# Four PSUM banks lent to the first and last side jobs of a Mamba phase, and its weight parts made in the phase ahead

## The chip, the cores and the metric

The kernel runs on one core of a Trainium2 chip. The metric is the device time of one execution in microseconds (us), and the value compared is the median of several runs. One run of the kernel before was also recorded by the hardware profiler; all times of single instructions come from that one.

The engines are called as in the profile: PE (TensorE, matrix products and transposes; PEld are its weight loads), DVE (VectorE), ACT (ScalarE), POOL (GpSimd) and SP (SyncE, which here issues every DMA). PE writes only to PSUM, whose eight banks hold 512 float32 numbers in each of 128 partitions.

## The reference, cut to what matters

The input is a batch of 8 feature maps of 256 channels, 32 by 32. Four layers follow each other: attention with a gated FFT feed-forward block; channel-group attention with a small MLP; an 8-bit quantised residual block of three convolutions; and a four-direction Mamba block. The change lies at the seam between the third and the fourth layer and at the end of the fourth, which computes for each of the four scan directions of each sample:

```python
xz = u @ W_in.T                                   # u: (1024, 256), W_in: (1024, 256)
x, z = jnp.split(xz, 2, axis=-1)
xc = conv1d_depthwise(x, conv_w, 4 taps) + conv_b
x = silu(xc)
x_dbl = x @ W_x.T                                 # 16 for dt, 16 for B, 16 for C
dt = softplus(x_dbl[..., :16] @ W_dt.T + b_dt)
A = -exp(A_log)                                   # 512 channels x 16 states
h_t = h_{t-1} * exp(dt_t A) + dt_t B_t x_t        # a scan over 1024 positions
y_t = sum over states of h_t C_t
y = (y + x * D) * silu(z)
out = y @ W_out.T
```

The four outputs, turned back to the layout of the image, are added.

## The kernel before

**Phase A** (`phase_a`) does layers 0 to 2 for all samples. Its last product is a tensor of 8-bit codes in DRAM for each sample. **Phase B** (`phase_b`) is the Mamba layer. The pools of the two phases use the same SBUF and PSUM, so that phase B starts when phase A has finished.

**The order of work.** In each phase every job is a Python generator ("strand") that yields its instructions one by one, or a condition that it waits for. The planner `_Order` holds for every instruction a cost and for every tile the time of its last use; at each step it picks, among the strands that are ready, the instruction that could start first, and between equals the one of the lowest rank. What it picks is emitted at once. On the chip each engine works through its own list strictly in this order, and SP its list of DMAs. Tiles come from a `_Room`, a fixed number of buffers of one shape; `take` waits until one is left. In phase A `fill` puts filler matmuls (tile `minus`) into the places where the planner sees PE waiting, one for every 0.3 us.

**Phase B** cuts the 1024 positions of each direction of each sample into two halves of 512. One half of one direction is a block; there are 64. A block has 16 groups, one for each state, and a group has four scans, one for each 128 channels. The stream of a block is: `scales` (ACT and POOL: dt·x times B, tile `dbu`), `turns` (PE: into bank `db`), `decays` (ACT: `da`), `scans` (DVE: `h`), `products` (POOL: times C, which `rows` loads into `cb`), `sums` (PE: adds over the states in four banks). The stream waits for nothing but its data; in its gaps the side jobs for later blocks run, which `ahead` hands to the planner at set places: `inputs` (the projections of W_in into `xi`), `mixed` (convolution, silu, W_x), `steps` (dt and `du`), and, after a sample's last direction, `fold` (the sums back to the channel layout), and `outputs` (the gate's projections, and W_out).

**The banks.** Phase B divides the eight banks so: `py_room` has 4, which `sums` holds for a block or a pair of blocks; `ps_room` (tag `db`) has 3; and `pp_room` has one, through which every side job passes:

```python
py_room = _Room(banks, "py", TH, [P, DI])
ps_room = _Room(banks, "db", 3, [P, HALF])
pp_room = _Room(banks, "pp", 1, [P, HALF])
```

**The head of phase B.** `W_in` is used as three bfloat16 parts, whose sum is the float32 weight. Ahead of everything else phase B loads each of the 8 pieces of 128 outputs (`da`), splits it on DVE (a cast, a subtraction, a cast, a subtraction, a cast, into `dbu`) and stores the parts to DRAM (`w_in`). A projection loads its parts from there into one of two `wi` tiles and multiplies them with `xf`, the codes of half an image as bfloat16, of which there is one tile. Then come `inputs` of the first sample (8 projections), `mixed(0)`, `steps(0)` and `mixed(1)`, all from the start and all through the one pp bank, and the stream begins when block 0 has its `du`.

**The tail.** After the last block's sums DVE adds the four py banks into `yT`, four folds follow (four transposes and one addition each), then for each half four gates (a projection, two instructions on DVE, three on ACT, one on POOL; two tiles `z`) and two products with W_out, each copied by ACT to a `z` tile and stored.

Most instructions of the phases are emitted by `_Op.emit`, so that the profile shows them all at line 132; they are told apart by their tiles. The loop that splits the weights is at lines 1163 to 1172.

## Time and profile before

| | us |
|---|---|
| median of 3 runs | 10775.12 |
| lowest and highest of them | 10765.92, 10776.5 |
| the profiled execution | 10771.94 |
| its span | 10770.2 |
| first DMA of phase B | 3683.84 |
| first projection | 3699.72 |
| first dbu | 3808.18 |
| first scan | 3811.12 |
| end of the last scan | 10708.15 |
| DVE's first addition of the last sums (yT) | 10711.78 |
| ACT's last copy | 10766.53 |

The span runs from the first to the last recorded instruction, and 1.7 us of the profiled time lie around it. Phase A takes the first 3683 us, the 64 blocks of the stream 6897 us (107.8 each), the head 127 us and the tail 59 us.

How to read the views: the page gives the busy time of each engine over the whole span, and a row of 40 slices. A table of windows gives the same for chosen stretches, with the clock that the throttle granted to PE (1.00 is full). The instructions in order of time show for each its start, its duration (of a run of equal ones, from the first start to the last end), and in brackets how long the engine had been idle before it and which instruction ended the wait. "pp<-xf,wi" writes tile pp from xf and wi.

### The profile page before, as it was taken

How to read it: one execution, taken by the hardware profiler on the slowest of the kernel's cores; microseconds unless marked ns; L12 is line 12 of the kernel's file. 1: busy time of each engine (PE TensorE's matmuls, PEld its weight loads, DVE VectorE, ACT ScalarE, POOL GpSimd, SP SyncE). 2: the span in 40 equal slices, each digit the busy share in tenths (PEclk: the TensorE clock that was granted, in tenths of full speed). 3: DMA queues.
4: the chain of work that ended last, by engine and by line, in shares of the span. 5: the costliest groups of instructions: out<-in, count | busy, mean ns of one | idle time of the engine just before them, and what ended most of it. 6: DMA issues, size and time to landing. Idle time of an engine off the chain costs nothing. (4 is left out here: it accounts for less than half of the span.)

```text
span 10770.2 us, 157247 instructions
## 1 busy us (share of the span) xinstructions
PE 9924.2 (92%) x58586; PEld 6252.6 (58%) x58698; DVE 8478.2 (79%) x8992; ACT 8690.8 (81%) x16283; POOL 6733.0 (63%) x3745
## 2 busy tenths in 40 slices
PE   9999999999999889999999999999989999999998
PEld 3333333333333267777777777777777777777776
DVE  5266557577665379898998998998899899899897
ACT  7867676777767488888888888888888888888887
POOL 1432133132220178888888888888888888888887
PEclk7988999989999899999999999999999999999999
DMA  1000000000000011111111111111111111111111
GB/s 46 29 18 16 22 16 22 13 22 12 13 13 10 30 41 39 50 48 50 48 46 52 50 41 55 41 50 53 44 49 52 47 48 46 52 50 43 55 41 47
DMA packets 217345, 410.00 MB, mean 38 GB/s; under 512 B 24881, under 2 KB 69297, under 8 KB 211458
## 3 DMA queue, kind: packets, MB, share of 16 engines
q1 hardware_dynamic: 216578, 399.94, 12.0%
q8 instruction: 461, 7.55, 0.3%
q14 instruction: 306, 2.51, 0.1%
HBM read 358.43 MB, written 30.93 MB: 36 GB/s over the span
## 5 line engine op out<-in xcount | busy, mean ns | idle before, releaser
L132 POOL TENSOR_TENSOR h<-h,cb 128x1024 f32<-128x1024 f32 x2048 | 4873.9, 2395 | 899.6 <-ACT st L132 445.5
L132 ACT ACTIVATE da<-dt,am 128x512 f32<-128x512 f32 x4096 | 2869.3, 713 | 505.9 <-DVE h L132 497.4
L132 DVE TENSOR_TENSOR_SCAN h<-da,st,db 128x512 f32<-128x512 f32 x2048 | 2467.2, 1257 | 167.9 <-PE db L132 92.7
L132 DVE TENSOR_TENSOR_SCAN h<-da,db 128x512 f32<-128x512 f32 x2048 | 2346.1, 1198 | 230.7 <-PE db L132 152.0
L132 ACT ACTIVATE dbu<-du,bT 128x512 f32<-128x512 f32 x3584 | 2474.9, 709 | 34.1 <-PE db L132 31.8
L132 PE MATMUL db<-ident,dbu 128*128 128x128 f32 x14336 | 2219.6, 280 | 165.0 <-DVE h L132 134.6
L132 PE MATMUL py<-ident,h 128*128 128x128 f32 x16384 | 2121.1, 275 | 93.9 <-POOL h L132 86.2
L132 PEld LDWEIGHTS db<-ident,dbu 128*128 128x128 f32 x14336 | 1672.9, 143 | 694.4 <-DVE h L132 364.2
L132 PEld LDWEIGHTS py<-ident,h 128*128 128x128 f32 x16384 | 1842.4, 141 | 171.5 <-POOL h L132 140.7
L132 DVE TENSOR_REDUCE stats<-bank 128x1 f32<-128x512 f32 x1536 | 981.5, 681 | 747.5 <-PE bank L132 746.4
L132 ACT ACTIVATE bank<-bank,stats 128x512 f32<-128x512 f32 x1536 | 1023.0, 669 | 391.2 <-DVE stats L132 380.9
L132 POOL TENSOR_TENSOR mid<-mid,mid 128x961 f32<-128x961 f32 (+2 forms) x192 | 401.2, 2097 | 1046.9 <-ACT mid L132 676.9
L132 PE MATMUL pp<-xi,cvd 128*128 128x512 f32 x2048 | 953.3, 609 | 9.6 <-ACT xs L132 3.4
L132 PE MATMUL bank<-big,big 32*128 32x512 f32 x4096 | 908.5, 670 | 36.5 <-ACT bank L132 17.9
L132 ACT ACTIVATE exps<-bank 128x512 f32<-128x512 f32 x1536 | 797.4, 621 | 137.6 <-PE bank L132 133.2
L132 PE MATMUL db<-dg,du 128*128 128x128 f32 x4096 | 811.0, 280 | 0.0
L132 POOL TENSOR_TENSOR dt<-dt,tmp 128x512 f32<-128x512 f32 x512 | 652.0, 1273 | 173.8 <-DVE tmp L132 151.0
L132 DVE TENSOR_TENSOR tmp<-dt,xs 128x512 f32<-128x512 f32 x256 | 604.2, 2360 | 194.3 <-POOL dt L132 194.1
L132 PEld LDWEIGHTS db<-dg,du 128*128 128x128 f32 x4096 | 638.0, 197 | 0.0
L132 PEld LDWEIGHTS pp<-xi,cvd 128*128 128x128 f32 x2048 | 380.8, 196 | 406.4 <-issue 391.9
L132 DVE SCALAR_TENSOR_TENSOR mid<-mid,cols,mid 128x961 f32<-128x961 f32 (+1 forms) x384 | 603.7, 1572 | 6.7
L132 PEld LDWEIGHTS bank<-big,big 32*128 32x128 f32 x4096 | 284.7, 192 | 499.2 <-issue 247.9
(186 smaller groups left out, 11280.3 us busy)
## 6 DMA issues: line engine op xcount, KB each, us to landing
cb<-c_d SPq DMA_DIRECT2D x1024, 256.0 KB, 3.2
wi<-w_in SPq DMA_DIRECT2D x192, 192.0 KB, 3.4
big<-in_x_dram SPq DMA_DIRECT2D x16, 1024.0 KB, 5.6
kept<-big SPq DMA_DIRECT2D x16, 1024.0 KB, 4.0
big<-kept SPq DMA_DIRECT2D x16, 1024.0 KB, 4.9
cdb<-codes SPq DMA_DIRECT2D x48, 256.0 KB, 4.1
big<-big SPq DMA_DIRECT2D x16, 512.0 KB, 7.2
out_dram<-z SPq DMA_DIRECT2D x32, 256.0 KB, 2.5
```

What stands on the lines that cost most here:

```text
L132: return getattr(getattr(nc, self.engine), self.method)(*self.args, **self.kw)
```

## The change

Phase A gets one strand more, `weight_parts`, of the lowest rank (9; the samples have 2). It does the loads, splits and stores of the weights that stood at the head of phase B, in two of phase A's seven `low` tiles, wherever the planner finds room. The DRAM tiles of the parts are made ahead of both phases.

In phase B a list `spare` decides which room a side job takes its bank from: `lend` takes from the four py banks as long as the list holds them, and from the single pp bank otherwise. It holds them from the start until block 0 has all its `du`, and again from the moment at which the last group's sums have left their banks. `sums` takes its four banks only when the first product of its block is there. `mixed(1)` is no longer started at once, but by `behind`, when block 0 has its `du` and the py banks are taken back. Every side job asks `lend` in place of `take(pp_room)`, and gives its bank back to the room that it came from.

```diff
-    phase_a(tc, i, col, ident, codes)
-    phase_b(tc, i, col, ident, codes, out)
+    parts = [dram.tile([P, CC, 3, P], BF16, name=f"w_in{m}", tag=f"w_in{m}") for m in range(2 * DC)]
+
+    phase_a(tc, i, col, ident, codes, parts)
+    phase_b(tc, i, col, ident, codes, parts, out)
...
+    def weight_parts():
+        for m, to in enumerate(w_parts):
+            w = yield from take(low, [P, CC, P])
+            o = yield from take(low, [P, CC, 3, P], BF16)
+            yield S.dma_start(w, i["w_in"].rearrange("(k p) m -> p k m", p=P)[:, :, m * P : (m + 1) * P])
+            for e in range(3):
+                yield V.tensor_copy(o[:, :, e], w)
+                if e < 2:
+                    yield V.tensor_tensor(w, w, o[:, :, e], ALU.subtract)
+            yield S.dma_start(to, o)
+            put(low, w)
+            put(low, o)
+
     with tc.manual_schedule():
         for b in range(B):
             order.add((2, b), sample(b))
+        order.add((9, B), weight_parts())
         order.run()
...
-    w_parts = [dr.tile([P, CC, 3, P], BF16, name=f"w_in{m}", tag=f"w_in{m}", bufs=1) for m in range(2 * DC)]
-    for m in range(2 * DC):
-        w, o = da_room.take([P, CC, P]), db_room.take([P, CC, 3, P], BF16)
-        nc.sync.dma_start(w, i["w_in"].rearrange("(k p) m -> p k m", p=P)[:, :, m * P : (m + 1) * P])
-        for e in range(3):
-            nc.vector.tensor_copy(o[:, :, e], w)
-            if e < 2:
-                nc.vector.tensor_tensor(w, w, o[:, :, e], ALU.subtract)
-        nc.sync.dma_start(w_parts[m], o)
-        da_room.put(w), db_room.put(o)
...
+    spare = [py_room]
+
+    def lend():
+        room = spare[0] if spare else pp_room
+        t = yield from take(room, [P, HALF])
+        return room, t
...
-            ps = yield from take(pp_room)
+            room, ps = yield from lend()
...
-            put(pp_room, ps)
+            put(room, ps)
...
             if s == 0 and fresh:
-                py = yield from takes(TH, py_room)
+                py = yield from takes(TH, py_room, when=lambda: (g, 0) in scaled)
...
                     put(py_room, py[t])
+                if g == len(groups) - 1:
+                    spare.append(py_room)
...
+    def behind(jobs):
+        d, h = blocks[0]
+        yield lambda: {("du", c) for c in range(DC)} <= d.done[h]
+        spare.clear()
+        for j in jobs:
+            order.add((0, 0), j)
+
-    for f in (list(inputs(0, False, xis[0, False])), mixed(0), steps(0), mixed(1)):
+    for f in (list(inputs(0, False, xis[0, False])), mixed(0), steps(0), [behind(mixed(1))]):
         for j in f:
             order.add((0, -1), j)
```

## The prediction

> **What bounds the kernel now.** I read the page first, then a table of windows by stage, then the instructions in order of time at the two places that the change touches.

> ```profile
> PE 9924.2 (92%) x58586; PEld 6252.6 (58%) x58698; DVE 8478.2 (79%) x8992; ACT 8690.8 (81%) x16283; POOL 6733.0 (63%) x3745
> ...
> PE   9999999999999889999999999999989999999998
> ```

> TensorE looks busy everywhere, but a slice is 269 us wide and hides both ends of the Mamba phase. The windows (engines in the header's order, then granted clock, DMA share and GB/s) show them:

> ```profile
> core 0: us, PE busy (x) PEld busy (x) DVE busy (x) ACT busy (x) POOL busy (x), PEclk, DMA share, GB/s
> 3683.80:3811.10 127.30, 78.00 (x168) 27.95 (x170) 30.19 (x70) 34.09 (x52) 31.51 (x45) 0.71 0.16 49
> 3811.10:3912.60 101.50, 92.01 (x622) 74.05 (x622) 86.78 (x78) 90.84 (x173) 82.96 (x46) 0.97 0.12 38
> 10421.40:10523.80 102.40, 92.81 (x642) 73.07 (x643) 94.68 (x83) 89.33 (x146) 90.03 (x50) 1.00 0.14 43
> 10523.80:10614.50 90.70, 78.98 (x593) 69.32 (x592) 88.47 (x81) 84.41 (x162) 86.55 (x47) 0.94 0.15 44
> 10711.70:10770.20 58.50, 33.97 (x98) 13.66 (x98) 17.87 (x24) 18.49 (x30) 10.12 (x8) 0.85 0.13 43
> ```

> The first row is the head: 127 us before the first scan, with every engine but TensorE three quarters idle. The last row is the tail, 58.5 us with all of them idle for long. The three between are single blocks of the stream (64 scans each), where four engines are near 90% and work is well overlapped. In head and tail one chain sets the time:

> ```profile
> 3683.84 2.43 SPq L1166 DMA_DIRECT2D da<-in_w_in_dram  x5
> ...
> 3699.72 0.59 PE L132 MATMUL pp<-xf,wi 128*128 128x512 bf16 x1 [31.88 <-DMA w_in<-dbu]
> ...
> 3703.28 2.72 PE L132 MATMUL pp<-xf,wi 128*128 128x512 bf16 x6 [0.84 <-DVE xi L132]
> ...
> 3739.67 3.67 PE L132 MATMUL pp<-xi,cvd 128*128 128x512 f32 x8 [0.87 <-ACT xs L132]
> ```

> ```profile
> 10715.90 1.11 PE L132 MATMUL pp<-ident,yT 128*128 128x128 f32 x4 [1.11 <-DVE ys L132]
> ...
> 10762.73 3.70 PE L132 MATMUL pp<-ys,w_o 128*128 128x512 f32 x8 [0.68 <-ACT z L132]
> ```

> Each bracket is a wait for the one pp bank: TensorE fills it, idles until DVE or ACT has emptied it, fills it again. The first bracket is another wait: the weight parts have to be split and stored before the first projection.

> **The change, part by part.** The profiled execution took 10771.94 us (span 10770.2), 3.2 below the median of 10775.12; I sum against the former and take the same difference off the median. The build's order of instructions says what moved: 48 projections, 16 conv matmuls, all of w_x, w_dt and transposes of block 0 now write py, and so do the tail's; DVE's order is the same from the third block to the end, bank names apart.

> *Head.* Before, from the timeline: start 3683.84, first projection 3699.72 (15.9), first conv 3728.39 (28.7), last xs done 3748.61 (20.2), xd done 3758.47 (9.9), first w_dt 3763.73 (5.3), last du done 3808.15 (44.4): 124.3 us.
> - Weight parts gone from here: 24 casts, 16 subtractions, 16 DMAs. SP issues w_x, w_o, w_dt (some 0.45 each), then cdb; its landing took 3.4 (3694.87 to 3698.23) and TensorE began 1.5 later. With 0.6 for the 512 KB of w_o ahead of it: 6.8 instead of 15.9. POOL's cvd, dd and memsets end at 3701.3, and the convs start after that: hidden.
> - Eight projections in four banks: DVE no longer gates them. At half clock 2.72 each back to back, plus 1.4 where the second half's xf is cast: 23.2. At full clock 1.46 each (as at 10731.16), but two wi tiles with a landing of 2.4 allow one per 2.0: 18.3 with a cold start. I take 20, plus 0.9 to the convs: 20.9 (28.7).
> - Convs: 4 x 3.67, then 0.7 for the last eviction: 15.4 (20.2). A cold start adds 2.2.
> - Table load 1.28, four silus 2.19, last w_x pair 0.9, xd 0.7, and 0.9 for half of a cold w_x (5.53 against 3.63): 6.0 (9.9). Transposes of xd: 0.5 (5.3, which held a conv of mixed(1)).
> - dt: one channel block goes w_dt to POOL's end in 6.2 (3763.73 to 3769.90), then multiply, transposes and copy, 0.7 each: 8.4. ACT needs 3.05 for each. tmp has three tiles and each takes two, so the third starts when the first is transposed (+7.7), the fourth some 3.3 later, and the last ends at 19.7. Bounds: 17.6 (ACT alone) to 26.9 (one after the other).

> Sum 69.3, so 55 less; 3 off for hand-overs that I don't see: **52** (42 to 58).

> *mixed(1) moved into block 0.* What filled the head's gaps now runs in the stream. Price by rows: the blocks at 10421.40 and 10523.80 both host a steps job, and only the first a mixed one: 102.4 against 90.7, so 11.7. The upper end is TensorE's own time, 4 x 3.67 + 3.63 = 18.3, since block 0 already has TensorE at 92.0 of 101.5 and would reach 110. The lower end is nothing, if it all falls into idle time. Queued behind its jobs are steps(1) and mixed(2), in the same bank. I take **14**, a third of the way up from the row.

> *Tail.* Four folds, each 2.2 apart, become DVE-bound at 1.06, so the gate projections start at 10718.1 instead of 10722.7. A gate's z goes DVE 0.75, ACT 1.95, POOL 1.26, some 4.1 with hand-overs, and z has two tiles. With that and the wi landings the fourth gate ends at 10730.6 (10740.0). The out projections take 0.9 + 3.7 (the first three quarters of the first are done by then), four more projections and gates follow to 10749.5, because the second store on SP now stands behind two wi loads and holds a z tile; then 0.9 + 3.7, copy 0.6 and store 3.1: 10758 instead of 10770.2. So **12**. At half clock throughout (2.72 and 5.5) I get 3.5; 15 if the store doesn't hold z.

> *Weight parts in the first phase.* By the rows 24 casts of 0.331 and 16 subtractions of 0.432, 14.9 us of DVE. By the order, part 0 stands ahead of the first layer norm (x lands at 20.5 to 25.7, DVE starts at 28.0), part 1 inside it, where DVE is the chain, parts 2 to 5 among the first softmax maxima, 6 and 7 at some 290 to 400 us, where DVE is nearly idle. SP gets 16 DMAs; its stores wait for DVE, and behind them stand two of the transfers big<-big. I count part 1 (1.9) and half of parts 2 to 5 (3.7): **6** lost. All of it exposed is 14.9. The clock also plays here:

> ```profile
> 100.00:230.00 130.00, 126.50 (x327) 40.92 (x324) 79.41 (x139) 102.31 (x271) 31.63 (x14) 0.61 0.06 16
> 230.00:480.00 250.00, 247.15 (x1250) 82.86 (x1248) 57.89 (x96) 203.15 (x365) 99.13 (x49) 1.00 0.12 32
> ```

> TensorE is the bound at a clock of 0.61; ten us more or less of half clock are worth 5. Ends: 8 gained, 20 lost. The two low tiles lent and 28 more filler matmuls show that this stretch's order shifts.

> 52 - 14 + 12 - 6 = **44 us**: 10728 in the profile, **10731** as median.

> [...] The row first, projections in one bank (clock in the third figure from the right):

> ```profile
> 3699.70:3728.30 28.60, 21.52 (x47) 0.50 0.20 59
> 3728.30:3732.80 4.50, 4.41 (x6) 0.50 0.00 0
> 3732.80:3766.90 34.10, 25.05 (x58) 1.00 0.09 25
> ```

> TensorE busy 75% of the time stayed at half clock for 28.6 us, and 4.5 us without a gap brought it to full. Back-to-back projections look like the second row, so I give them the full clock after some 4 us. [...]

> **The rivals.**
> 1. *The first phase takes it back.* All 14.9 us of DVE exposed and 30 us more of half clock at 100 to 300 us: 30 lost instead of 6, gain 20, 10755. For: DVE is in the chain from 28 to 50 us. Against: after 50 us it waits 95 us for TensorE in the first 300.
> 2. *Block 0 chokes on its one bank.* Hold times: conv 4.5, w_x 5.3 with its transposes, dt 4.6. Two mixed and one steps make 65 us of a block of 115; if the busy engines stretch each hold 2.2 times, 140, and block 1 waits 25 us: gain 19, 10756. Against: blocks with inputs, mixed and steps pass in 107.5.
> 3. *Slower: the clock drops in the first attention.* From 230 to 480 us TensorE is busy 247 of 250 us at clock 1.00. Every us of that at half clock costs half a us. From 132 of the 250 us on, 66 are lost and the kernel is 22 slower: 10797. Against: the order there is nearly the same and DVE has 58 of 250 us busy.

> That the change doesn't do what it says is excluded by the order.

> **How the numbers follow.** A measurement tells 0.2%, 21.5 us, from no change. Forecast 0.82; rival 1 0.07, rival 2 0.06 (both within 0.2%), rival 3 0.05. Half-widths: head 8, block 0 9, tail 6, first phase 14; together, as independent, 19, stretched to 26 to take in the two rivals inside 0.2%: 10706 to 10758.

> **What would show it.** Right: first projection some 7 us after the phase's first DMA; projections without waits for DVE xi; first scan some 50 us sooner after that DMA; block 0 at 113 to 118 us; the last store some 46 us after the last sums. Wrong: the phase's first DMA later than 3700 (rival 1); a wait of DVE scans for dbu or du ahead of block 1 (rival 2); a clock below 1.00 between 230 and 480 (rival 3).

## The result, and the profile after

The changed kernel took 10706.29 us (median of four runs, 10696.43 to 10710.81); the kernel before, run beside it, took 10775.81. The ratio is 0.9939, with a 95% interval of 0.9923 to 0.9955: faster by 0.6%, as forecast in sign. The forecast time of 10731 was 25 us too long, and the measured one lies at the very low end of the range (10706). The profiled execution of after took 10710.81 us (span 10708.9), the longest of the four.

The page of after, its first line of busy times and its row of PE slices, to set against the first fence of the prediction:

```profile
PE 9899.2 (92%) x58614; PEld 6251.0 (58%) x58726; DVE 8487.3 (79%) x8991; ACT 8702.0 (81%) x16284; POOL 6736.6 (63%) x3746
...
PE   9999999999999899899999999999989999998998
```

It hardly shows a change: the same work, the same shares, the row ends in 8998 where it ended in 9998. The gain lies again in stretches much shorter than a slice. The windows of head, block 0 and tail of after (columns as before):

```profile
core 0: us, PE busy (x) PEld busy (x) DVE busy (x) ACT busy (x) POOL busy (x), PEclk, DMA share, GB/s
3674.80:3747.30 72.50, 47.42 (x130) 19.37 (x132) 15.93 (x27) 24.90 (x39) 25.75 (x43) 0.77 0.17 50
3747.30:3857.10 109.80, 103.53 (x650) 75.40 (x648) 91.05 (x82) 97.54 (x181) 83.34 (x46) 1.00 0.11 35
10666.30:10708.90 42.60, 32.25 (x97) 14.42 (x97) 17.68 (x24) 18.21 (x30) 10.16 (x8) 0.87 0.19 59
```

The head shrank from 127.3 to 72.5 us, the tail from 58.5 to 42.6. Block 0 grew from 101.5 to 109.8, with TensorE now busy for 103.5 of it: the convolutions that left the head are there. Put together from the two profiles:

| stage (us) | before | after | gain | forecast |
|---|---|---|---|---|
| first phase, up to the first DMA of phase B | 3683.8 | 3674.9 | 9.0 | -6 |
| head, to the first scan | 127.3 | 72.4 | 54.8 | 52 |
| blocks 0 to 3 | 418.8 | 432.8 | -14.0 | -14 |
| blocks 4 to 63 | 6478.2 | 6482.6 | -4.4 | 0 |
| from the last scan's end to the end | 62.1 | 46.2 | 15.8 | 12 |
| sum | 10770.2 | 10708.9 | 61.3 | 44 |

The instructions of after's head in order of time, PE's and SP's first one:

```profile
3674.85 0.38 SPq L1173 DMA_DIRECT2D w_x<-in_w_x_dram  x1
...
3682.51 0.59 PE L134 MATMUL py<-xf,wi 128*128 128x512 bf16 x1 [23.67 <-ACT xf L134]
...
3690.07 1.47 PE L134 MATMUL py<-xf,wi 128*128 128x512 bf16 x6 [1.01 <-DMA wi<-w_in]
3692.30 1.46 PE L134 MATMUL py<-xf,wi 128*128 128x512 bf16 x6 [0.75 <-ACT xf L134]
...
3699.15 13.90 PE L134 MATMUL py<-xi,cvd 128*128 128x512 f32 x32
...
3741.06 5.64 PE L134 MATMUL pp<-xi,cvd 128*128 128x512 f32 x8
3746.54 0.49 PE L134 MATMUL db<-ident,dbu 128*128 128x128 f32 x3
```

The brackets have changed. In before they named DVE or ACT, emptying the one bank; now the projections wait for their weights (`wi`) and for the cast of the input (`xf`), and the four convolutions run as one row of 32 matmuls without a gap. One bracket in the head still reads `[0.81 <-DVE xi]`, ahead of the seventh projection at 3696.20; the weight load that starts with it waited for `wi`, and with two banks the wait at this place reads `[0.66 <-DMA wi]`, so it too goes with the weights. The last two lines show something that the forecast lacked: a convolution of `mixed(1)`, released when block 0 has its `du`, got onto TensorE's list ahead of the first `db`, so that the first scan comes 5.3 us after the last `du`, where it came 3.0 after it before.

In the tail, gate products and out products follow each other without bank waits. The two longest waits of DVE now end when a store frees a `z` tile:

```profile
10669.35 4.10 DVE L134 TENSOR_TENSOR ys<-py,ys 128x512 f32<-128x512 f32 x4 [0.57 <-PE py L134]
...
10679.45 7.26 PE L134 MATMUL py<-ys,w_o 128*128 128x512 f32 x16
...
10688.60 0.75 DVE L134 TENSOR_SCALAR z<-py,cols 128x512 f32<-128x512 f32 x1 [6.78 <-DMA out_dram<-z]
...
10692.69 0.75 DVE L134 TENSOR_SCALAR z<-py,cols 128x512 f32<-128x512 f32 x1 [2.67 <-DMA out_dram<-z]
```

Of the 6.78 only some 0.6 are the store's: up to 10686.7 TensorE was at the out products, and the projection that this gate reads ended at 10688.0. The 2.67 are the store's whole.

### The profile page after: what moved, and what is told of

Same layout as the page of the kernel before. It is cut to its first block, busy times and chain, and to the rows that moved or that the text cites. A ratio compares the mean times of both kernels' runs of the same rounds, so it can differ in the third digit from the quotient of the medians.

```text
span 10708.9 us, 157325 instructions
## 1 busy us (share of the span) xinstructions
PE 9899.2 (92%) x58614; PEld 6251.0 (58%) x58726; DVE 8487.3 (79%) x8991; ACT 8702.0 (81%) x16284; POOL 6736.6 (63%) x3746
## 5 line engine op out<-in xcount | busy, mean ns | idle before, releaser
L134 PE MATMUL pp<-xi,cvd 128*128 128x512 f32 x2016 | 930.6, 605 | 3.5 <-DVE dt L134 1.5
```

The costliest lines, as they stand in the source:

```text
L134: return getattr(getattr(nc, self.engine), self.method)(*self.args, **self.kw)
```

## The experiments

The profiles left three questions. Which part of the head's gain is the banks', which the weights', and which the later `mixed(1)`? Is the shorter first phase the weights' doing, or only a luckier execution? And why did TensorE's clock come up so much sooner than in before (1.47 us for each projection from the fourth on, where all eight of before took 2.72)?

Theory A: the terms are separate, and the weight parts in the first phase cost nothing there, since their order also changes how long TensorE runs at half clock. Rival B: the shorter first phase is the spread between executions. Rival C: the weight work is hidden wherever it stands. Rival D: the blocks after the head are slower for another reason than the moved work. All stages of all whole kernels, from one profile each (us):

| kernel | first phase | head | blocks 0-3 | blocks 4-63 | after the last scan |
|---|---|---|---|---|---|
| before | 3683.8 | 127.3 | 418.8 | 6478.2 | 62.1 |
| warm-up only | 3670.9 | 121.1 | 419.4 | 6484.6 | 62.2 |
| weights only | 3677.3 | 109.6 | 419.1 | 6488.2 | 62.5 |
| banks only | 3702.7 | 81.6 | 426.4 | 6478.7 | 44.5 |
| mixed(1) at once | 3687.9 | 82.6 | 422.7 | 6477.9 | 44.6 |
| after | 3674.9 | 72.4 | 432.8 | 6482.6 | 46.2 |
| weights late | 3691.3 | 71.4 | 426.4 | 6485.4 | 45.7 |
| two banks | 3672.0 | 72.9 | 426.4 | 6474.9 | 45.0 |
| wide | 3665.8 | 68.0 | 426.4 | 6478.9 | 38.6 |

Head and tail repeat within 1 or 2 us between kernels that share their code there. The first phase does not: before, warm-up only and banks only have the same instructions in it in the same order, and took 3683.8, 3670.9 and 3702.7 us. So totals are compared as ratios to runs of before beside them (whose median was 10760.55 in one group and 10776.83 in another), and stages by the profile.

**Weights only.** The parts are made in the first phase; head and tail keep their one bank, and `mixed(1)` starts at once.

```diff
-        room = spare[0] if spare else pp_room
+        room = pp_room
...
-                py = yield from takes(TH, py_room, when=lambda: (g, 0) in scaled)
+                py = yield from takes(TH, py_room)
...
-    for f in (list(inputs(0, False, xis[0, False])), mixed(0), steps(0), [behind(mixed(1))]):
+    for f in (list(inputs(0, False, xis[0, False])), mixed(0), steps(0), mixed(1)):
```

> Only the weight parts move to the first phase; every side job keeps the one bank. Theory A (the three terms are separate, and the first phase is shorter because the shifted order at its start brings the full clock earlier): the first phase has the changed kernel's order, so it is 9 us or more shorter than before again; the head loses the wait for the split weights, 15.9 down to 7.7; blocks and tail as before. Total 10776 - 9 - 9 = 10758, down to 10750. Rival B (the 9 us of the first phase were one execution's luck, and the weight work costs the 6 us that I forecast): 10776 + 6 - 9 = 10773.

Measured: 10761.13 us, ratio 0.9989 (0.998 to 0.9998). The head is 17.7 us shorter than before's, where the first projection comes only 8.2 sooner (7.65 us after the phase's first DMA instead of 15.9). Nearly all of the rest is TensorE's clock. The projections in order of time:

```profile
3684.94 2.72 PE L134 MATMUL pp<-xf,wi 128*128 128x512 bf16 x6 [23.65 <-ACT xf L134]
3688.50 1.45 PE L134 MATMUL pp<-xf,wi 128*128 128x512 bf16 x6 [0.84 <-DVE xi L134]
3690.80 1.46 PE L134 MATMUL pp<-xf,wi 128*128 128x512 bf16 x6 [0.84 <-DVE xi L134]
```

One bank, the same wait of 0.84 us for DVE as in before, and yet 1.46 us each from the second on, where all eight of before took 2.72: 19.8 us to the first convolution instead of 28.7. The clock of the profiles changes on a grid of 3.41 us: of the 224 stretches of one clock in before's records and the 216 in after's, all but the last of each, which the end of the record cuts off, are whole multiples of 3.413 us long. Windows on that grid, first of before, then of weights only (a step is "filled" by the share of it in which matmuls ran):

```profile
3702.09:3705.51 3.42, 2.58 (x7) 0.83 (x6) 0.75 (x1) 0.00 (x0) 0.00 (x0) 0.50 0.22 58
3705.51:3708.92 3.41, 2.57 (x7) 0.70 (x6) 0.75 (x1) 0.00 (x0) 0.00 (x0) 0.50 0.42 135
```

```profile
3684.80:3688.22 3.42, 2.72 (x6) 0.87 (x7) 0.53 (x1) 0.48 (x1) 3.42 (x7) 0.50 0.00 0
3688.22:3691.63 3.41, 2.29 (x10) 0.96 (x10) 0.97 (x2) 0.00 (x0) 2.25 (x13) 1.00 0.36 102
3691.63:3695.04 3.41, 2.08 (x9) 0.68 (x7) 1.21 (x2) 0.41 (x1) 0.00 (x0) 1.00 0.45 148
```

Before filled its steps to 0.75 and stayed at half clock; this kernel's first projection happened to fall whole into one step, filled it to 0.80, and the steps after it were at full clock with only 0.61 to 0.67 filled. So 8.8 of the 17.7 us in this one profile come with a clock that rose after the first projection; whether its place on the grid decided it was not shown. The total is nearer to A's 10758 than to B's 10773, but not for A's reasons: in the profile the first phase is 6.5 us shorter (A: 9 or more), the head 17.7 (A: 9), and blocks 4 to 63 are 10.0 longer.

**Banks only.** The weight parts are made at the head of phase B again, all else as in after.

```diff
-        order.add((9, B), weight_parts())
...
+    for m in range(2 * DC):
+        w, o = da_room.take([P, CC, P]), db_room.take([P, CC, 3, P], BF16)
...
+        da_room.put(w), db_room.put(o)
```

> Only the banks are lent; the weight parts are made at the head of the Mamba phase as before, and the first phase has the order of before. Theory A: head 55 less the 8 that the weights were worth, so 47 gained; blocks 0 to 3 lose 14 to 18; tail gains 16; first phase nothing: 10776 - 47 + 16 - 16 = 10729. Rival B gives the same here; if the total comes out at 10715 or below, the first phase's part of the gain isn't the weights' doing at all.

Measured: 10707.5 us (10703.74 to 10735.7), ratio 0.9944 (0.9931 to 0.9957). The head is 81.6 us, so that the weights' part of after's head is 9.2 us (the forecast's 15.9 to 6.8 is 9.1). By the expectation's rule a total of at most 10715 spoke against the weights having shortened the first phase. But the profiled execution is the slowest of the five, with a first phase of 3702.7 us, so that this total could not decide it; the runs of the first phase alone, below, were made for that.

**Weights late.** The strand waits until the fifth sample has passed its first stage.

```diff
     def weight_parts():
+        yield lambda: stage[4] >= 1
```

> The changed kernel, but the weight parts wait until sample 4 has passed its first layer, so that the first phase starts in the order of before. Theory A (order at the start sets the clock there): the half clock of the first 250 us comes back to some 123 us from 99, and the first phase is 9 or more longer than in the changed kernel: 10716 to 10722. Rival C (the weight work is simply hidden wherever it stands, and the first phase is faster for another reason): as the changed kernel, 10706.

Measured: 10728.99 us (10710.41 to 10747.42), ratio 0.9963 (0.9949 to 0.9976). Head and tail are those of after; the first phase took 3691.3 us. C, by which the place of the work makes no difference, expects after's time; this is 23 us above it. It is also above A's 10716 to 10722, and A's reason did not show: TensorE was at half clock for 96 us of the first 250, not for some 123 (after: 99).

**mixed(1) at once.** The four banks are lent, but the convolutions of block 1 start with those of block 0.

```diff
-    for f in (list(inputs(0, False, xis[0, False])), mixed(0), steps(0), [behind(mixed(1))]):
+    for f in (list(inputs(0, False, xis[0, False])), mixed(0), steps(0), [behind([])], mixed(1)):
```

> The changed kernel, but mixed(1) starts at once again, now through the four lent banks. Theory A (a mixed job moved into the stream costs 11.7 to 18.3 us, its price in blocks 0 to 3 was 14): blocks 0 to 3 are back to 101.6, 107.5, 106.6, 103.1, and the head grows by mixed(1)'s work on PE (18.3) where that isn't hidden in the dt chain's gaps, so by 5 to 18: total 10697 to 10710. Rival D (blocks 0 to 2 are slower because the whole stream starts differently, not because of mixed(1)): the blocks stay at 109.8, 112.0, 108.3 and the total rises to 10711 to 10724.

Measured: 10709.0 us (10699.98 to 10717.5), ratio 0.9943 (0.9931 to 0.9955). The head is 10.2 us longer than after's, blocks 0 to 3 are 10.1 shorter than after's and 3.7 shorter than those of the four other kernels that move the work. Almost all of this is block 0, 100.4 us against 109.8 in the kernels that move the work, so that D is out there. Blocks 1 to 3 stay at 322.3 us, with four single steps at half clock, much as in after (323.0, also four); the four other kernels, without such a step, took 316.6. The move alone is worth nothing that a total can show. Against weights only, where just the banks differ, the head lost 27.0 us: this is what the four banks are worth there, the largest single part of the change. With the 17.7 of weights only and the 10.2 of the move it makes up the 54.8 us of the head. The split depends on the order in which the parts are added: banks only, less the same 10.2, gives the banks 35.5, and the 8.5 more are close to the 8.8 that the clock was worth in weights only.

**Two banks.** As after, but with only two of the four py banks lent.

```diff
-    spare = [py_room]
+    two = _Room(banks, "py", 2, [P, DI])
+    spare = [two]
...
-                    spare.append(py_room)
+                    spare.append(two)
```

> After, with only two of the four py banks lent to the side jobs of head and tail. Theory A (two banks are enough, one being filled while the other is emptied: an eviction of 0.6 to 0.75 us is shorter than any product): head 72 to 75 us (72.4 with four), tail 46 to 49 us (46.2). Rival (four are needed because DVE and ACT fall behind in bursts): head 78 us or more, as the dt chain holds a bank from w_dt to the eviction by DVE three steps later. Total within 5 us of after by A, 8 or more above it by the rival.

Measured: 10694.2 us, ratio 0.9944 (0.993 to 0.9957); head 72.9, tail 45.0 us. The rival that four are needed is out. The timeline has the rows of after's, but for one wait more in the dt chain (0.82 us, for DVE's `dt`); one bank is filled while the other is emptied:

```profile
3689.22 1.46 PE L134 MATMUL py<-xf,wi 128*128 128x512 bf16 x6 [0.75 <-ACT xf L134]
...
3696.17 13.90 PE L134 MATMUL py<-xi,cvd 128*128 128x512 f32 x32
```

**Warm-up only.** Before, with ten idle matmuls after each split weight piece, so that TensorE does not idle ahead of the first projection.

```diff
+    warm = py_room.take([P, HALF])
     for m in range(2 * DC):
...
+        for _ in range(10):
+            nc.tensor.matmul(warm[:, : 3 * P], lhsT=o[:, 0, 0], rhs=o[:, 0].rearrange("p e m -> p (e m)"), start=True, stop=True)
...
+    py_room.put(warm)
```

> Before, with one thing added: ten matmuls of 128x384 into an idle py bank after the split of each of the eight weight pieces, on data that is there anyway and with a result that nobody reads. They fill the 32 us in which TensorE idles ahead of the first projection. Still one pp bank and the same waits for DVE. [...] Rival (the changing bank itself keeps the clock down): the projections fall back to 2.72 within a few, and the head keeps its 127 us.

Measured: ratio 0.9999 (0.999 to 1.0009); the effect of a few us is below what totals show, and the trace has to be read:

```profile
3675.64 15.18 PE L1174 MATMUL py<-dbu 128*128 128x384 bf16 x80 [20.77 <-DMA w_x<-in_w_x_dram]
3690.66 1.46 PE L132 MATMUL pp<-xf,wi 128*128 128x512 bf16 x5
3692.96 1.46 PE L132 MATMUL pp<-xf,wi 128*128 128x512 bf16 x6 [0.84 <-DVE xi L132]
```

With one bank and all its waits the eight projections run at 1.46 us, 18.6 us to the first convolution instead of 28.7, at a clock of 1.00. So the rival is out: through the same bank, with the same waits of 0.84 us, the projections ran at 0.50 in before, with matmuls in 21.5 of 28.6 us (0.75), and run at 1.00 here, with matmuls in 11.65 of 18.6 us (0.63). This fits weights only, where seven of the eight took 1.46 us. The head gained only 6.2 us, since the added matmuls end at 3690.8 and put the first projection 3.9 us later behind the phase's first DMA.

**The first phase alone.** Three kernels without the Mamba phase: one without the strand of the weight parts, so with the order of before, one with it at the start, as in after, and one with it late, by the wait shown above. The first two ran in two groups.

```diff
-    phase_b(tc, i, col, ident, codes, parts, out)
+    last = ctx.enter_context(tc.tile_pool(name="last", bufs=1))
+    none = last.tile([P, HALF], F32, name="none", tag="none")
+    nc.vector.memset(none, 0.0)
+    for b in range(B):
+        for k in range(CC):
+            for h in range(2):
+                nc.sync.dma_start(out[b, k * P : (k + 1) * P, h * HALF : (h + 1) * HALF], none)
```

> Leaves out the Mamba phase (zeros are stored as its output) and the weight parts: the first phase alone, in the order of before. In two profiles this same order took 3683.8 us (before) and 3702.7 us (the banks without the weights), so all theories expect a median near 3690 us plus some 45 us for the stores of zeros, and single runs 20 to 30 us apart, since instructions and order are the same every time.

> Also without the Mamba phase, but the first phase makes the weight parts, as in after. To be read against the run of the first phase alone. Theory A (the weight work is hidden, and the shifted order lets TensorE's clock drop less): 9 to 15 us shorter in the median, as the profiles of after and of the weights alone (3674.9, 3677.3) stand to 3683.8 and 3702.7. Rival B (the difference of the profiles is only the spread between executions): within 5 us. The forecast on record: 6 us longer.

> The first phase alone in the order of before, once more, for the spread: the first five runs were 3697.9 to 3713.5, median 3711.6. If the order sets the clock (theory A), the median is again 3705 or more; if it is spread between executions, it can as well be 3695.

> The first phase alone with the weight parts, once more: the first four runs were 3693.6 to 3707.9, median 3695.9. Theory A: 8 to 16 us below the other order run beside it. Rival B: within 5 us of it. The forecast on record: 6 above it.

> The first phase alone, with the weight strand held back until the fifth sample is through its first stage, where DVE and SP have the most idle time; this order in the whole kernel gave 10729 against 10706 with the strand at the start. Theory A (the granted clock follows the order of the first 700 us, not the work): near the order without the weights, 10 to 20 us above the strand at the start. Theory C (the work itself is the price, and late it is hidden): the same as the strand at the start or less.

| first phase alone (us) | median | lowest and highest | ratio to before in its group, interval |
|---|---|---|---|
| without the weights, first group | 3711.62 | 3697.85, 3713.45 | 0.3447 (0.3441 to 0.3453) |
| weights at the start, first group | 3695.87 | 3693.58, 3707.9 | 0.3437 (0.3432 to 0.3442) |
| without, second group | 3714.58 | 3707.84, 3720.34 | 0.3445 (0.3438 to 0.3451) |
| weights at the start, second group | 3706.91 | 3699.29, 3710.93 | 0.3437 (0.3431 to 0.3443) |
| weights late, second group | 3729.9 | 3725.95, 3736.02 | 0.3459 (0.3454 to 0.3465) |

At the start the weights make the phase 15.8 and 7.7 us shorter in the two groups by the medians, 10.3 and 8.3 by the means; the intervals of each pair overlap a little, but 6 us longer, as forecast, fits neither. Late they make it 15.3 us longer than none and 23.0 longer than at the start, beyond both ranges. So C is out, B with its 5 us is unlikely, and A stands for the sign, though not for its reason in the late variant. The whole kernels agree: 3675.6 us on the mean of five with the weights at the start, 3685.8 of three without. Banks only, whose total by this should be some 19 us above after's and was 1 above, is the one result that does not fit; with single runs 32 us apart it can be spread, which was not shown.

The profiles part in the first attention. The stretch from 100 to 230 us (clock in the third figure from the right) in after, then in the first phase alone without the weights (second group):

```profile
100.00:230.00 130.00, 128.40 (x447) 46.10 (x444) 83.75 (x146) 110.69 (x296) 27.11 (x12) 0.75 0.13 28
```

```profile
100.00:230.00 130.00, 127.49 (x416) 43.29 (x414) 86.64 (x161) 112.52 (x300) 31.62 (x14) 0.74 0.12 27
```

TensorE is busy for 98% or more of it in both. Before, and the first phase with the weights late, had 0.61 in the same order that has 0.74 here, so that one profile tells little. With the weights at the start all seven profiles reached the 257th of DVE's 1536 maxima (a point that the order of work fixes) between 576 and 591 us; without them the five profiles reached it at 596 to 613. At the last of the maxima 10.4 of that mean lead of 26 us were left.

The two late kernels reached the 257th maximum at 601 and 608 us, within the range of those without the strand. They fell behind on the way to the 513th, in which their strand runs (876 to 1096 us): 631 us each, where those without it took 615 to 622. The stretch from 950 to 1100 us in the first phase alone, without the weights (second group) and with them late:

```profile
950.00:1100.00 150.00, 146.29 (x695) 48.91 (x697) 104.86 (x172) 120.49 (x315) 7.57 (x6) 0.90 0.00 1
```

```profile
950.00:1100.00 150.00, 148.17 (x577) 45.87 (x577) 118.87 (x204) 112.78 (x302) 7.58 (x6) 0.78 0.05 16
```

So the late strand does not cost its time at the start, as A had it, but mostly here, at a lower clock. The kernels with the strand at the start take 629 to 630 us from the 257th to the 513th as well, and lose half of their lead there, with no weight work left; why is not shown.

**Wide.** What after still waits for in head and tail is tiles, and the stream's own are idle there. While the banks are lent, `wi` and `xf` come from the ten `dbu` tiles and `z` from the five `da` tiles.

```diff
-        xf = yield from take(xf_room)
+        wide = db_room if spare else xf_room
+        xf = yield from take(wide, [P, CC, HALF], BF16)
...
-        w = yield from take(wi_room)
+        wide = db_room if spare else wi_room
+        w = yield from take(wide, [P, CC, 3, P], BF16)
...
-            t = yield from take(z_room)
+            wide = da_room if spare else z_room
+            t = yield from take(wide)
...
```

> After, and while the py banks are lent (head and tail) the side jobs also take their other tiles from the stream's idle rooms: wi and xf from the ten dbu tiles, z from the five da tiles, in place of two, one and two. Theory A (what is left in after's head and tail are the waits for wi, xf and z): the projections lose the waits of 1.01, 0.75, 0.18, 0.18, 0.81 and 0.17, so the head is 69 to 71 us (72.4); in the tail the waits of 6.78 and 2.67 for a z tile held by a store go, and the time from the last scan's end to the end is 38 to 42 us (46.2), limited next by ACT (eight gates of 1.96) and by the out projections (7.3 for each half). Total 6 to 11 us below after. Rival (TensorE's clock falls in the tail and the out projections take it back): tail 45 or more.

Measured: 10686.77 us, ratio 0.9917 (0.99 to 0.9933); head 68.0, tail 38.6 us. In order of time, the projections of the head, then of the tail, ACT's gates, and the last out products:

```profile
3673.36 12.40 PE L134 MATMUL py<-dbu,dbu 128*128 128x512 bf16 x48 [23.54 <-ACT dbu L134]
...
10648.10 10.48 PE L134 MATMUL py<-dbu,dbu 128*128 128x512 bf16 x42
...
10651.69 13.01 ACT L134 ACTIVATE da<-da 128x512 f32<-128x512 f32 x21 [12.85 <-DVE da L134]
...
10666.58 7.03 PE L134 MATMUL py<-ys,w_o 128*128 128x512 f32 x16
```

All 48 projection matmuls of the head stand in one row of 12.4 us (after: 16.6), and ACT works through seven of the tail's eight gates without a pause. The rival that the clock takes it back is out (0.90 in this tail, 0.87 in after's). This version beats both kernels: before clearly by its interval, after by 4.4 us in the head and 7.6 in the tail of the profiles, while the two intervals of the ratios still overlap. The medians lie 19.5 us apart, where 6 to 11 were expected; head and tail account for 12.0 of them, and the profile's first phase (3665.8 us) is again 9.0 shorter with the same instructions.

## Why the prediction was right, and where it was off

The mechanism of head and tail was right, and their sizes came near. That the time fell inside the range, and by 0.3 us, was luck: the first phase went the other way than forecast, and the four executions of after alone lie 14 us apart.

**Head, 52 forecast, 54.8 measured.** Step by step: start to first projection 7.7 us (6.8 forecast); projections 16.6 (20.9); convolutions to the last xs 14.6 (15.4); to the end of xd 6.3 (6.0); to the first w_dt 0.1 (0.5); the dt chain to the last du 21.9 (19.7). The sum to the last `du` is 67.1 (69.3). The term most off is the projections: I gave them a start in the cold and a mean between 18.3 and 23.2, and they rose to 1.47 us from the fourth on and were then paced by the landing of `wi`, as the bracket of 1.01 shows. The 3 us taken off for unseen hand-overs were right in size (2.3) though not in kind: they are the convolution of `mixed(1)` ahead of the first `db`.

**mixed(1) moved, -14 forecast, -14.0 in after's profile.** That it fits is partly chance. Four other kernels with the same move lost 7.6 in blocks 0 to 3; after's own lost 6.4 more in block 1, 2 and 3, where its clock fell for four single steps of 3.41 us, and in the two-bank kernel not once. Block 0 took 109.8 us, not the 113 to 118 that I had named as a sign. The row of nearest work (11.7) was too high for the usual case.

**Tail, 12 forecast, 15.8 measured.** The store held `z`, as said (some 0.6 and 2.67). What was undersized: of both out products three quarters were done ahead of the last gate, not of the first alone, so the first pair ended 20.4 us after the additions of the last sums began (23.4 by the forecast's steps), and that lead of 3 us stayed to the end (42.6 us instead of 46.2).

**First phase, 6 lost forecast, some 8 to 16 gained.** This step failed in sign, and its end of 8 gained was too near. I counted part 1 and half of parts 2 to 5 as lost on DVE. DVE in order of time, first one line of before, then one of after:

```profile
43.00 0.69 DVE L132 SCALAR_TENSOR_TENSOR low<-low 128x512 f32<-128x512 f32 x1 [1.11 <-ACT low L132]
```

```profile
41.51 0.29 DVE L134 CAST low<-low 128x256 bf16<-128x256 f32 x1
```

Part 1 went into the time in which DVE had waited for ACT, and the first maximum of the softmax came at 47.3 us instead of 50.7. I priced the instructions and left the clock, which I had named as worth 5 us for ten, as a symmetric risk. In the first 600 us the seven profiles with the weights at the start were at half clock for 131 us in the mean, the five without for 170; at half a us each that is an estimated 20 of the lead of 26. Up to 3660 us it is 575 against 585, worth 5 of the 10.4 that are left, and the other half stays unexplained. The late variant shows that rival 1 was a real danger: the same work elsewhere costs 15 us.

**The rivals.** Rival 1 is out here: the phase's first DMA came at 3674.85, not after 3700. (The sign was a weak one, as 3702.7 in banks only came with before's order; the runs of the first phase alone decide.) Rival 2 is out: block 1's first scans follow block 0's without a wait for `dbu` or `du`. What block 0 did do is wait for TensorE (scans for `db` and for the sums of `h` behind convolutions: 16.0 and 8.6 us in blocks 0 and 1, before 7.5 and 0.5). Rival 3 is out: clock 1.00 from 230 to 480 us in both.

**The clock row.** I gave back-to-back projections the full clock after some 4 us, from the stretch of 4.5 us without a gap after which before was at 1.00. In after, with four banks cycled, the clock was at 0.50 up to 3687.1, 4.6 us after the first projection began, and at 1.00 for the 37 us after that; six matmuls took 1.47 us from the fourth projection on, and the head's clock was 0.77 against 0.71. My own row, "75% busy stayed at half clock", was read as a property of the one bank; warm-up only, at 1.00 with 63% busy, shows that the same waits can go with either clock.

## What to carry to other kernels

Where one buffer is handed round between two engines at the ends of a kernel, borrow a second from the stream that has not started or has ended: here the second brought nearly all of it (a head of 72.9 us with two banks, 72.4 with four), and the next wait is then for the other tiles of the same jobs, which can be borrowed alike. Read a clock next to a duration: in weights only half of the head's gain (8.8 of 17.7 us) came with projections at a clock of 1.00 where before's had 0.50, and such a half need not come back in the next version. When single executions of an unchanged stage differ by 30 us (here 3670.9 to 3702.7), cut the stage out and time it alone before giving it a cause.
